# Last attention: key sums between the key blocks, four-tile scores, triangles on GpSimd and scalings on VectorE

## The chip, the cores and the metric

The kernel runs on one core of one Trainium2 chip. The metric is the device time of one execution in microseconds, as the median of several runs; lower is better. The engines are called as in the profile: PE (TensorE's matmuls) with PEld (its weight loads), DVE (VectorE), ACT (ScalarE), POOL (GpSimd) and SP (SyncE).

## The reference

The model is a chain of eight small layers on two batches of 1024 tokens with 256 channels, in float32. The change lies in the seventh stage's attention alone, which adds to the residual stream `x` a local attention of 16 heads of 64 channels. Each query block of 128 tokens sees its own and the two neighbouring key blocks, within 127 tokens, and besides them 64 "side" keys, each the sum of 16 consecutive tokens. The softmax has an extra logit of zero.

```python
bl = LOCAL_RADIUS + 1            # 128
nb = L // bl                     # 8 blocks
G = L // TOKENS_PER_BLOCK        # 64 sums of 16 tokens
q = einsum('bld,dhk->blhk', x, Wq) / sqrt(dh)
k = einsum('bld,dhk->blhk', x, Wk)
v = einsum('bld,dhk->blhk', x, Wv)
g = einsum('bld,lg->bgd', x, one_hot)          # sums of 16 tokens
side_k = einsum('bgd,dhk->bghk', g, Wk)
side_v = einsum('bgd,dhk->bghk', g, Wv)
k_cat = concatenate([three_blocks(k), side_k])
v_cat = concatenate([three_blocks(v), side_v])
logits = einsum('bnqhd,bnkhd->bnhqk', qb, k_cat)
valid = (abs(rel) <= 127) & (k_pos >= 0) & (k_pos < L)
logits = logits + where(valid, 0, -1e9)        # side keys: no bias
m = maximum(max(logits), 0)
p = exp(logits - m) / (sum(exp(logits - m)) + exp(-m))
y = einsum('bnhqk,bnkhd->bnqhd', p, v_cat)
out = einsum('blhk,hkd->bld', y, Wo)
```

A query and a key at the same place of neighbouring blocks are 128 apart and so not valid. Hence for one query, of the two neighbour blocks together, exactly 127 keys count: those after its place in the block before, and those ahead of its place in the block behind. The kernel uses that: it merges both neighbours into one block of 128 columns.

## The kernel before

The whole program is one stream of instructions written in Python; a scheduler of the language orders the instructions of each engine by when it thinks their inputs are ready, so their order on an engine isn't quite that of the text. `attn1` runs the last attention once for each batch, in two stages.

*Projection.* For each of eight groups `m` of 128 channels (two heads), `pq` holds the keys of 512 tokens (L1499) and ACT copies it to `kT` (L1500). The 64 key sums are a product of their own, `pg`, from the summed tokens `g` (L1505), copied to `sk`. Then come the values `pv` (L1513), copied to `v` by DVE and ACT in turn, and the value sums `sv` (L1527). In the second batch the steps of the next stage's adapter (`adapter2_steps`) run beside the keys.

*Heads.* `attn1_heads` walks over items `(n, m)`: eight query blocks `n`, and in each four items of two pairs of heads. `staggered` issues for each item `scores`, for the item before it `turn`, and for the one before that `values`. Twice in eight items a block of PE work stands between: `queries` projects the queries of two blocks (L1565), and DVE scales them into `qT` (L1572); `output` applies the output weights (L1689).

- `scores`, per pair of heads: both heads lie in the upper and lower 64 rows. A product of 64x128 weights with 384 keys each (L1598), one with the 64 sums each (L1602), in the PSUM tile `ps`, one bank a head. In inner blocks (`0 < n < 7`) DVE merges the neighbours with a predicated copy of 128x128 for each head (L1604, L1605, mask `near`). One instruction of DVE adds the mask `wbs`, negates and takes the row's minimum (L1608); ACT takes the exponential and its sum (L1618). With the extra logit (L1622) DVE forms the reciprocal (L1624, L1625). DVE scales the first head of the pair (L1626) and ACT the second (L1627).
- `turn`: PE transposes the probabilities into `pt` (own block, merged neighbours; L1640) and `pts` (sums; L1641). ACT copies the own block (L1644) and the sums (L1650). In inner blocks DVE splits the merged neighbours by multiplying `pt` with each of two triangles `tri` (L1647).
- `values`: products with `v` and `sv` for each head on 128x64 tiles (L1667), a copy on ACT (L1679).

PSUM in the heads' stage: `ps` twice two banks, `pt0`, `pt1`, `pts` and `py` one bank each, eight in all.

Of the kernel before, what the change touches and what calls it, by code (L numbers as in the profile page):

```python
# [9 lines left out]
F32 = mybir.dt.float32  # L10
# [8 lines left out]
P = 128  # L19
# [43 lines left out]
def tiles(tc, **how):  # L63

    return tc.tile_pool(reuse_waits="tile", **how)
# [1355 lines left out]

def load_attn1(k, pool, names):
    for n in names:
        k.w1a[n] = pool.tile([P, 2048], F32, name=f"w1a{n}")
        k.nc.sync.dma_start(out=k.w1a[n], in_=part(k.ins["w1a"], W1A, n))


def attn1(k, ci, x):
# [7 lines left out]
    with tiles(tc, name="a1r", bufs=1) as rp:  # L1436
# [6 lines left out]
        wbs = rp.tile([P, 4, G + 2 * P + G], F32, name="wbs")  # L1443
# [12 lines left out]
        left, right = slice(G, G + P), slice(G + P, G + 2 * P)  # L1456
        for t, op, sign in (
            (wbs[:, 0, right], ALU.is_gt, -1),
            (wbs[:, 1, right], ALU.not_equal, 1),
            (wbs[:, 2, left], ALU.not_equal, 1),  # L1460
            (wbs[:, 3, left], ALU.is_gt, 1),
        ):
            nc.gpsimd.affine_select(
                out=t, in_=t, compare_op=op, fill=-1.0e9, base=0, pattern=[[sign, P]], channel_multiplier=-sign
            )

        near = rp.tile([P, 2, P], U8, name="near")
        for i, t in enumerate((wbs[:, 3, left], wbs[:, 0, right])):
            nc.vector.tensor_scalar(near[:, i], t, 0.0, None, ALU.is_ge)
        for b in range(B):  # L1470
            kT = rp.tile([P, 8, S], F32, name="kT")
            v = rp.tile([P, NB, 1024], F32, name="v")

            g = rp.tile([P, 2, 2, G], F32, name="g")
            sk = rp.tile([P, 8, G], F32, name="sk")

            sv = rp.tile([P, 8, 2, 64], F32, name="sv")
            nc.gpsimd.memset(sv, 0.0)
            for c in range(2):
                nc.vector.reduce_sum(  # L1480
                    g[:, c, 0, :], ci[:, c, b * S : (b + 1) * S].rearrange("p (g t) -> p g t", t=16), axis=AX.X
                )
            nc.vector.tensor_copy(g[:, :, 1, :], g[:, :, 0, :])
            with ExitStack() as st:
                pp = st.enter_context(tiles(tc, name="a1a", bufs=2 if b else 3, space=PSUM))
# [6 lines left out]
                for m in range(8):  # L1492
                    ms = slice(m * P, (m + 1) * P)
                    for half in range(2):
                        ts = slice(b * S + half * CK, b * S + (half + 1) * CK)
                        ls = slice(half * CK, (half + 1) * CK)
                        pq = pp.tile([P, CK], F32, name="pq")
                        for c in range(2):
                            nc.tensor.matmul(pq, lhsT=wk[:, c, ms], rhs=ci[:, c, ts], start=c == 0, stop=c == 1)  # L1499
                        nc.scalar.copy(kT[:, m, ls], pq)  # L1500
                    if beside:
                        next(beside[m // 4])
                    pg = pp.tile([P, G], F32, name="pg", bufs=1 if b else 2)
                    for c in range(2):
                        nc.tensor.matmul(pg, lhsT=wk[:, c, ms], rhs=g[:, c, 0, :], start=c == 0, stop=c == 1)  # L1505
                    nc.vector.tensor_copy(sk[:, m, :], pg)
                for half in range(2):
# [17 lines left out]
                    for i in range(2):  # L1525
                        rows = slice(i * G, (i + 1) * G)
                        nc.vector.tensor_copy(  # L1527
                            sv[rows, 4 * half : 4 * half + 4, i],
                            pv[rows].rearrange("p (m i d) -> p m i d", i=2, d=64)[:, :, i],
                        )  # L1530
            with (
# [4 lines left out]
                attn1_heads(k, b, x, ci, kT, v, sk, sv, (wbs, near, tri), rp, sp, pp, yp)  # L1536


def attn1_heads(k, b, x, ci, kT, v, sk, sv, masks, rp, sp, pp, yp):
# [18 lines left out]
    def queries(n):  # L1558

        qT = rp.tile([P, 8, 2 * P], F32, name="qT", bufs=2)  # L1560
        for m in range(0, 8, 4):
            pq = pp.tile([P, 4, 2 * P], F32, name="ps")
# [9 lines left out]
            nc.vector.tensor_scalar_mul(qT[:, m : m + 4, :], pq, 0.125)  # L1572
        rows["qT", n // 2] = qT

    def scores(it):
# [5 lines left out]
        k0 = max(0, n - 1) * P  # L1581
        nk = 3 * P if inner(n) else 2 * P
        hps = [slice(64 * i, 64 * i + 64) for i in range(2)]

        keys = (slice(3 * P - nk, 3 * P), slice(G, G + nk))
        sums = (slice(3 * P, 3 * P + G), slice(0, G))
        used = (slice(P, P + W), slice(0, W))
        it["pe"] = []  # L1590
        for pair in range(2):
# [4 lines left out]
            qs = [rows["qT", n // 2][hp, m + pair, (n % 2) * P : (n % 2 + 1) * P] for hp in hps]  # L1596
            for i, hp in enumerate(hps):
                nc.tensor.matmul(  # L1598
                    ps[:, i, keys[i]], lhsT=qs[i], rhs=kT[hp, m + pair, k0 : k0 + nk], start=True, stop=True
                )  # L1600
            for i, hp in enumerate(hps):
                nc.tensor.matmul(ps[:, i, sums[i]], lhsT=qs[i], rhs=sk[hp, m + pair, :], start=True, stop=True)  # L1602
            if inner(n):
                nc.vector.copy_predicated(ps[:, 0, 2 * P : 3 * P], near[:, 0], ps[:, 0, 0:P])  # L1604
                nc.vector.copy_predicated(ps[:, 1, G : G + P], near[:, 1], ps[:, 1, G + 2 * P : G + 3 * P])  # L1605
            for i in range(2):

                nc.vector.tensor_tensor_reduce(  # L1608
                    out=pe[:, i],
                    in0=ps[:, i, used[i]],  # L1610
                    in1=wbs[:, 0 if n == 0 else 3 if n == NB - 1 else 1 + i, (1 - i) * G : (1 - i) * G + W],
# [4 lines left out]
                    accum_out=nm[:, i : i + 1],  # L1616
# [342 lines left out]
```

## Time and profile before

| | |
|---|---|
| median of 3 runs | 1522.83 us (1522.0 to 1526.31) |
| profiled execution | 1529.71 us, span 1528.0 us |
| mean granted clock of TensorE | 0.949 |
| PE busy | 1428.8 us, 94% |
| DVE busy | 873.6 us, 57% |
| ACT busy | 681.2 us, 45% |
| POOL busy | 180.7 us, 12% |
| L1598, products of queries with keys | 512 records, 110.1 us busy |
| L1608, mask and minimum | 256, 118.6 us, 487 ns each |
| L1647, triangles | 96, 64.8 us, 675 ns each |
| L1626 / L1627, scalings on DVE / ACT | 128 each, 48.8 / 70.8 us |
| L1604 / L1605, predicated copies | 96 each, 27.9 / 28.4 us |

Busy time is the union of an engine's records; a mean is that of a record. A float32 product leaves two records (two passes), each with its own weight load. Records of one engine can overlap, so the distance between two starts says more about an engine's pace than the length of a record. The times in the profile are microseconds from the start of the span.

### The profile page before, as it was taken

How to read it: one execution, taken by the hardware profiler on the slowest of the kernel's cores; microseconds unless marked ns; L12 is line 12 of the kernel's file. 1: busy time of each engine (PE TensorE's matmuls, PEld its weight loads, DVE VectorE, ACT ScalarE, POOL GpSimd, SP SyncE). 2: the span in 40 equal slices, each digit the busy share in tenths (PEclk: the TensorE clock that was granted, in tenths of full speed). 3: DMA queues.
4: the chain of work that ended last, by engine and by line, in shares of the span. 5: the costliest groups of instructions: out<-in, count | busy, mean ns of one | idle time of the engine just before them, and what ended most of it. 6: DMA issues, size and time to landing. Idle time of an engine off the chain costs nothing. (4 is left out here: it accounts for less than half of the span.)

```text
span 1528.0 us, 27342 instructions
## 1 busy us (share of the span) xinstructions
PE 1428.8 (94%) x10778; PEld 973.6 (64%) x10778; DVE 873.6 (57%) x2774; ACT 681.2 (45%) x1681; POOL 180.7 (12%) x167
## 2 busy tenths in 40 slices
PE   5998989999699999968999989999999999999998
PEld 2445977455556666645666544788887557888866
DVE  3545733121399931157887712788784237878764
ACT  2343143222122222217888721666565427656733
POOL 1523630022411121110000010000000000000011
PEclk8799578999889999979999999999999999999999
DMA  9500003300243432030000020000000000000001
GB/s 302 189 1 2 5 2 118 159 30 30 82 149 131 140 111 98 18 121 1 2 2 2 1 84 0 2 2 2 1 2 2 0 1 2 2 1 2 2 14 42
DMA packets 42757, 70.75 MB, mean 46 GB/s; under 512 B 7168, under 2 KB 35840, under 8 KB 39552
## 3 DMA queue, kind: packets, MB, share of 16 engines
q1 hardware_dynamic: 35776, 55.55, 10.8%
q0 software_dynamic: 3072, 8.65, 1.6%
q10 hardware_dynamic: 3776, 4.75, 0.9%
q8 instruction: 86, 1.41, 0.4%
q14 instruction: 47, 0.39, 0.1%
HBM read 45.09 MB, written 23.86 MB: 45 GB/s over the span
## 5 line engine op out<-in xcount | busy, mean ns | idle before, releaser
L1618 ACT ACTIVATE pe<-pe,nm 128x320 f32<-128x320 f32 x256 | 141.9, 555 | 131.1 <-DVE nm L1608 131.0
L1608 DVE CUSTOM_DVE_ANT_0 pe<-ps,wbs 128x320 f32<-128x320 f32 x256 | 118.6, 487 | 6.1 <-PE ps L1602 1.8
L1230 ACT ACTIVATE pe<-pe,nm 128x256 f32<-128x256 f32 x256 | 110.4, 498 | 20.6 <-DVE nm L1220 20.6
L965 PE MATMUL ph<-xt,w 128*128 128x512 f32 x256 | 114.0, 603 | 2.7 <-ACT xt L960 2.7
L1598 PE MATMUL ps<-kT,qT 64*128 64x384 f32 (+1 forms) x512 | 110.1, 498 | 3.3 <-DVE qT L1572 2.9
L973 PE MATMUL po<-w,h 128*128 128x256 f32 x512 | 111.8, 379 | 0.0
L973 PEld LDWEIGHTS po<-w,h 128*128 128x128 f32 x512 | 97.3, 190 | 16.6 <-issue 3.3
L1220 DVE CUSTOM_DVE_ANT_0 pe<-ps,lc 128x256 f32<-128x256 f32 x256 | 94.2, 417 | 21.1 <-PE ps L1204 19.5
L1667 PE MATMUL py<-ptt,v 128*64 128x128 f32 x1408 | 103.6, 277 | 0.1
L895 DVE SCALAR_TENSOR_TENSOR lc<-iok,idx,lc 128x256 f32<-128x256 f32 x248 | 102.1, 474 | 0.3
L965 PEld LDWEIGHTS ph<-xt,w 128*128 128x128 f32 x256 | 48.7, 193 | 62.8 <-issue 55.9
L1667 PEld LDWEIGHTS py<-ptt,v 128*64 128x64 f32 x1408 | 78.7, 137 | 11.1 <-issue 8.1
L1640 PE MATMUL pt<-ident,pe 128*128 128x128 f32 x512 | 79.8, 281 | 1.9 <-DVE pe L1626 0.9
L1239 PE MATMUL ptp<-ident,pe 128*128 128x128 f32 x512 | 73.7, 282 | 5.7 <-DVE pt L1243 3.6
L1239 PEld LDWEIGHTS ptp<-ident,pe 128*128 128x128 f32 x512 | 55.5, 141 | 33.5 <-ACT pe L1230 17.2
L968 ACT ACTIVATE h<-ph,vecs 128x512 f32<-128x512 f32 x64 | 44.0, 687 | 71.3 <-PE ph L965 71.3
L1627 ACT ACTIVATE pe<-pe,rd 128x320 f32<-128x320 f32 x128 | 70.8, 558 | 9.0 <-DVE rd L1625 8.9
L1602 PEld LDWEIGHTS ps<-sk,qT 64*128 64x128 f32 x512 | 50.9, 187 | 26.2 <-issue 0.3
L1499 PE MATMUL pq<-c,w1ak 128*128 128x512 f32 x128 | 60.1, 612 | 5.5 <-ACTq L1844 5.5
L1647 DVE TENSOR_TENSOR ptt<-pt,tri 128x512 f32<-128x512 f32 x96 | 64.8, 675 | 0.0
L1640 PEld LDWEIGHTS pt<-ident,pe 128*128 128x128 f32 x512 | 56.2, 141 | 10.9 <-issue 2.0
L976 DVE TENSOR_TENSOR ye<-po,b 128x256 f32<-128x256 f32 x32 | 13.4, 418 | 82.0 <-PE po L973 82.0
(355 smaller groups left out, 2769.8 us busy)
## 6 DMA issues: line engine op xcount, KB each, us to landing
w<-in_mw SPq DMA_DIRECT2D x16, 1024.0 KB, 5.5
xs<-z SPq DMA_DIRECT2D x8, 1088.0 KB, 11.7
ys<-z SPq DMA_DIRECT2D x4, 1024.0 KB, 11.6
xe<-xs SPq DMA_DIRECT2D x7, 544.0 KB, 6.2
more<-xs SPq DMA_DIRECT2D x7, 544.0 KB, 3.9
x<-in_xT ACTq DMA_DIRECT2D x4, 512.0 KB, 5.9
g<-ys ACTq DMA_DIRECT2D x4, 512.0 KB, 5.9
out_x<-o SPq DMA_DIRECT2D x8, 256.0 KB, 2.1
```

Source lines behind the costliest of these rows:

```text
L895: nc.vector.scalar_tensor_tensor(n, key, k.idx[:, qb, j : j + 1], n, ALU.is_equal, ALU.add)
L965: nc.tensor.matmul(ph, lhsT=w1[:, c, m * P : (m + 1) * P], rhs=xt[:, c, :], start=c == 0, stop=c == 1)
L973: nc.tensor.matmul(po, lhsT=h[:, m, j * P : (j + 1) * P], rhs=w2[:, m, :], start=m == 0, stop=m == 7)
L1220: nc.vector.tensor_tensor_reduce(out=pe[:, j, :], in0=it["ps"][i][:, j, :], in1=k.lc[:, q0 + j, :], scale=-1.0, scalar=3.0e38, op0=ALU.add ...
L1230: nc.scalar.activation(pe[:, j, :], pe[:, j, :], AF.Exp, bias=nm, scale=-1.0)
L1239: nc.tensor.transpose(ptp[:, kb, j, :], it["pe"][i][:, j, kb * P : (kb + 1) * P], k.ident)
L1598: nc.tensor.matmul(ps[:, i, keys[i]], lhsT=qs[i], rhs=kT[hp, m + pair, k0 : k0 + nk], start=True, stop=True)
L1608: nc.vector.tensor_tensor_reduce(out=pe[:, i], in0=ps[:, i, used[i]], in1=wbs[:, 0 if n == 0 else 3 if n == NB - 1 else 1 + i, (1 - i) * G ...
L1618: nc.scalar.activation(pe[:, i], pe[:, i], AF.Exp, bias=nm[:, i : i + 1], scale=-1.0, accum_out=den[:, i : i + 1])
L1627: nc.scalar.activation(pe[:, 1], pe[:, 1], AF.Copy, scale=rd[:, 1:2])
L1640: nc.tensor.transpose(pt[1 - j if i and inner(n) else j][:, 2 * pair + i, :], pe[:, at : at + P], k.ident)
L1667: nc.tensor.matmul(py[64 * i : 64 * i + 64, (m + pair) % 4, :], lhsT=keys[:, hs], rhs=it["pts"][:, pair, :] if j == 3 else it["pt"][:, j, ...
```

## The change

Five things are changed together.

1. *Layout of the keys.* `kT` holds 1280 columns for 1024 keys: between the key blocks lie copies of the 64 key sums, three in the rows of the first head of each pair and four in those of the second (`KEYS`). For every query block one contiguous stretch holds the keys it needs and one copy of the sums. A head's view has the sums in the middle or at an edge; `window(n)` gives for both heads where the stretch starts, which columns are used and which are merged into which (`place`, `merge`, `kind`, `masked`, `parts`).
2. *Key sums.* The product `pg` goes. DVE sums `pq` over 16 tokens into `sk`, and GpSimd copies `sk` into its places in `kT`, once every four groups. The copies of `pq` to `kT` are split at the gaps: ACT copies the first head's 64 rows, DVE the second's.
3. *Scores.* Each pair has four products: two heads by two halves of 64 queries, each on a tile of 64x64, with 320, 384 or 448 columns. A half of the queries leaves out the 64 columns of a neighbour in which it has no valid key. The products with the sums go. In inner blocks the predicated copy of 128 columns becomes two of 64 columns, one on all rows and one on 64 rows.
4. *Triangles.* ACT copies the merged block from `pt[1]` as it is; GpSimd multiplies the copy with each triangle in SBUF.
5. *Scalings.* DVE scales both heads of a pair; ACT none.

Besides, `qT` becomes three buffers of four groups in place of two of eight, the `pq` tile has three buffers in both batches, `wbs` has three masks in place of four, and `sv` is held twice, with its two halves exchanged, since which head's sums come first now depends on the block.

The diff, cut to its core:

```diff
+class Keys:
+    def __init__(self, order):
+        self.at, self.sums, at = {}, [], 0
+        for n in order:
+            if n is None:
+                self.sums.append(at)
+                at += S // 16
+            else:
+                self.at[n] = at
+                at += P
...
+KEYS = [Keys([0, 1, None, 2, 3, None, 4, 5, None, 6, 7]), Keys([None, 0, 1, 2, None, 3, 4, None, 5, 6, 7, None])]
+
+def window(n):
+    first = 0 if n == 0 or n in (1, 3, 5) else 1
+    return [KEYS[i].view(i, n, first ^ i) for i in range(2)]
...
-                        nc.scalar.copy(kT[:, m, ls], pq)
+                        gs = slice(half * G // 2, (half + 1) * G // 2)
+                        nc.vector.reduce_sum(sk[:, m, gs], pq.rearrange("p (g t) -> p g t", t=16), axis=AX.X)
+                        for i in range(2):
+                            hp = slice(64 * i, 64 * i + 64)
+                            for n0, n1 in KEYS[i].runs(4 * half, 4 * half + 4):
+                                at, w = KEYS[i].at[n0], (n1 - n0) * P
+                                o = (n0 - 4 * half) * P
+                                copy = nc.vector.tensor_copy if i else nc.scalar.copy
+                                copy(kT[hp, m, at : at + w], pq[hp, o : o + w])
...
-                    for c in range(2):
-                        nc.tensor.matmul(pg, lhsT=wk[:, c, ms], rhs=g[:, c, 0, :], start=c == 0, stop=c == 1)
-                    nc.vector.tensor_copy(sk[:, m, :], pg)
+                    if m % 4 == 3:
+                        for i in range(2):
+                            hp = slice(64 * i, 64 * i + 64)
+                            for at in KEYS[i].sums:
+                                nc.gpsimd.tensor_copy(kT[hp, m - 3 : m + 1, at : at + G], sk[hp, m - 3 : m + 1])
...
                     for i in range(2):
-                        rows = slice(i * G, (i + 1) * G)
-                        nc.vector.tensor_copy(
-                            sv[rows, 4 * half : 4 * half + 4, i],
...
+                        for j in range(2):
+                            rows = slice((i ^ j) * G, ((i ^ j) + 1) * G)
+                            nc.vector.tensor_copy(
+                                sv[rows, j, 4 * half : 4 * half + 4, i],
...
-            for i, hp in enumerate(hps):
-                nc.tensor.matmul(
-                    ps[:, i, keys[i]], lhsT=qs[i], rhs=kT[hp, m + pair, k0 : k0 + nk], start=True, stop=True
-                )
-            for i, hp in enumerate(hps):
-                nc.tensor.matmul(ps[:, i, sums[i]], lhsT=qs[i], rhs=sk[hp, m + pair, :], start=True, stop=True)
-            if inner(n):
-                nc.vector.copy_predicated(ps[:, 0, 2 * P : 3 * P], near[:, 0], ps[:, 0, 0:P])
-                nc.vector.copy_predicated(ps[:, 1, G : G + P], near[:, 1], ps[:, 1, G + 2 * P : G + 3 * P])
+            for half in range(2):
+                qs = slice((n % 2) * P + half * 64, (n % 2) * P + half * 64 + 64)
+                for hp, view in zip(hps, views):
+                    c0, c1 = view.parts[half]
+                    nc.tensor.matmul(
+                        ps[hps[half], view.head, c0:c1],
+                        lhsT=rows["qT", n // 2, m // 4][hp, (m + pair) % 4, qs],
+                        rhs=kT[hp, m + pair, view.start + c0 : view.start + c1],
+                        start=True,
+                        stop=True,
+                    )
+            for view in views:
+                i, j = view.head, view.place
+                if inner(n):
+                    to, of = view.merge
+                    both, one = (slice(0, 64), slice(64, P)) if view.kind == 0 else (slice(64, P), slice(0, 64))
+                    for rs, cs in ((slice(0, P), both), (one, one)):
+                        nc.vector.copy_predicated(
+                            ps[rs, i, to + cs.start : to + cs.stop],
+                            near[rs, view.kind, cs],
+                            ps[rs, i, of + cs.start : of + cs.stop],
+                        )
...
-            nc.vector.tensor_scalar_mul(pe[:, 0], pe[:, 0], rd[:, 0:1])
-            nc.scalar.activation(pe[:, 1], pe[:, 1], AF.Copy, scale=rd[:, 1:2])
+            for j in range(2):
+                nc.vector.tensor_scalar_mul(pe[:, j], pe[:, j], rd[:, j : j + 1])
...
         if inner(n):
-            for i in range(2):
-                nc.vector.tensor_mul(ptt[:, 1 + i], pt[1], tri[:, i : i + 1, :].to_broadcast([P, 4, P]))
+            nc.scalar.copy(ptt[:, 1], pt[1])
+            for i in (1, 0):
+                nc.gpsimd.tensor_mul(ptt[:, 1 + i], ptt[:, 1], tri[:, i : i + 1, :].to_broadcast([P, 4, P]))
```

## The prediction

> **What bounds the kernel now.** The page comes first, for the engines' shares:
>
> ```profile
> PE 1428.8 (94%) x10778; PEld 973.6 (64%) x10778; DVE 873.6 (57%) x2774; ACT 681.2 (45%) x1681; POOL 180.7 (12%) x167
> ```
>
> PE looks like the bound, but these are means over all stages. The change lies in the last attention, from 890 to 1465 us, so I read one steady step there (two pairs of heads), first PE in the timeline:
>
> ```profile
> 1319.94 0.92 PE L1598 MATMUL ps<-kT,qT 64*128 64x384 f32 x4
> 1320.68 0.34 PE L1602 MATMUL ps<-sk,qT 64*128 64x64 f32 x4
> 1320.85 0.87 PE L1598 MATMUL ps<-kT,qT 64*128 64x384 f32 x4
> 1321.55 0.33 PE L1602 MATMUL ps<-sk,qT 64*128 64x64 f32 x4
> 1321.82 0.65 PE L1640 MATMUL pt<-ident,pe 128*128 128x128 f32 x4
> ...
> 1324.96 0.92 PE L1598 MATMUL ps<-kT,qT 64*128 64x384 f32 x4
> ```
>
> The columns are start, length, engine, line, tiles, count. A step takes PE 5.02 us (1319.94 to 1324.96) without a gap: scores 1.88, transposes 1.24, values 1.90. Now DVE over the same time:
>
> ```profile
> 1321.38 0.29 DVE L1604 COPY_PREDICATED ps<-near,ps 128x128 f32<-128x128 uint8 x1
> ...
> 1324.49 0.67 DVE L1647 TENSOR_TENSOR ptt<-pt,tri 128x512 f32<-128x512 f32 x1
> 1325.08 0.38 DVE L1626 TENSOR_SCALAR pe<-pe,rd 128x320 f32<-128x320 f32 x1
> 1325.37 0.68 DVE L1647 TENSOR_TENSOR ptt<-pt,tri 128x512 f32<-128x512 f32 x1
> 1326.01 0.16 DVE L1624 TENSOR_TENSOR rd<-den,extra 128x2 f32<-128x2 f32 x1
> 1326.41 0.39 DVE L1626 TENSOR_SCALAR pe<-pe,rd 128x320 f32<-128x320 f32 x1
> 1326.71 0.28 DVE L1604 COPY_PREDICATED ps<-near,ps 128x128 f32<-128x128 uint8 x1
> ```
>
> One turn of DVE takes 5.33 us (1321.38 to 1326.71), longer than PE's step. DVE falls behind 0.31 us a step and is saved because after every four steps PE works 7.1 us on queries (L1565) or 7.5 on the output (L1689), where DVE catches up. Four steps and such a block are a "burst": two bursts took 55.28 us (1297.38 to 1352.66), one 27.64.
>
> When does DVE decide? PE's transposes in a burst's fourth step need the third turn of DVE. With a turn D, DVE starting L after the burst, then 0.15 hand-over, 0.62 transposes of the last pair, 1.90 values, 7.3 block and 0.26 (half of the 0.52 us after each query block), a burst lasts L + 3D + 10.23. With L = 1.13 (scores at 1314.92, first copy at 1316.05) and D = 5.33 that is 27.35, only 0.29 below the measured 27.64. **PE bounds the bursts, but DVE stands right behind it.**
>
> **The change part by part.**
>
> *Scores.* The products with the key sums (L1602) go; the four products of a pair now lie on four 64x64 tiles. A quarter tiling already runs:
>
> ```profile
> 144.86 0.34 PE L412 MATMUL sc<-ru,k 64*64 64x64 f32 x8 [0.15 <-DVE A L420]
> ```
>
> Eight records of 0.22 to 0.27 us fit in 0.34, so four run at once. A pass of 384 columns takes 0.32 us; two passes a pair, two pairs, first load and the switch to transposes (0.15) make 1.5 to 1.6 us against 1.88. I take 0.35 saved, a PE step of 4.67. In blocks 1 and 6 a tile has 448 columns (0.05 longer a pass, 0.2 a step), which doesn't matter if DVE bounds. In blocks 0 and 7 (320 columns) some 0.25 is saved a step; no triangles lie there, and of these 16 steps in all I leave out four that only fill the pipe: 12 x 0.25 = 3 us.
>
> *DVE's turn.* Starts lie apart as follows: L1647 0.59 and 0.64, L1626 0.30, predicated copies 0.325. The triangles go: -1.23. Two scalings come from ACT: +0.60. Four copies of 128 columns become eight of 64: 64 elements fewer are 0.067 less at the 1.04 ns an element of DVE's rows (128x512 0.68, 128x256 0.42), so 8 x 0.26 = 2.08 against 1.30: +0.78 (ends: 8 x 0.20, +0.3; 8 x 0.325, +1.3). D = 5.33 - 1.23 + 0.60 + 0.78 = 5.48. L becomes 0.90 (no sums to wait for). Burst: 0.90 + 16.44 + 10.23 = 27.57. PE alone would do 27.64 - 4 x 0.35 = 26.24, so **the 1.4 us that PE gains stay hidden behind DVE**: -0.07 a burst.
>
> Half of those copies' views start at row 64. Row first: the two sv copies (L1527), rows 0 and 64, start 0.43 us apart though the first is 0.416 long, while 256-wide products (L463) start 0.335 apart at 0.419 long. [...]
>
> *POOL.* Two products of 128x512 per step, in SBUF, come after an ACT copy. Nearest rows: L309, in place, 1.09 us; L202 1.26. Together about 2.2 us, one behind the other. In themselves they are free: PE has the values of the step before, the next scores and transposes (about 4.7 us) to do before it needs them, against 0.5 + 2.2. What they cost is DVE:
>
> ```profile
> 1473.40 1.40 POOL L223 TENSOR_TENSOR both<-nsq 128x512 f32<-128x512 f32 x1 [101.06 <-ACT nsq L221]
> 1473.72 3.31 DVE L1731 SCALAR_TENSOR_TENSOR xk<-df,vecs,c 128x512 f32<-128x512 f32 x2
> 1474.76 1.72 POOL L202 TENSOR_TENSOR both<-x 128x512 f32<-128x512 f32 x1
> 1476.44 2.34 POOL L1755 TENSOR_TENSOR ka<-ka 128x1024 f32<-128x1024 f32 x1
> 1476.95 3.04 DVE L1731 SCALAR_TENSOR_TENSOR xr<-df,vecs,c 128x512 f32<-128x512 f32 x2
> ```
>
> These DVE instructions take 0.74 us alone. Beside POOL two took 3.31 and the next 2.38: each waited for POOL's running product, ran 0.55, and POOL took the next turn. DVE rows that read PSUM and one SBUF tile (L308 beside L309, 0.74) show nothing of it. Which of ours are exposed? By the row, those with two SBUF inputs: the additions L1624, two a step; that is W = 0.3 us a turn at most. [...] The closest the trace has is L497, a copy in SBUF: 0.54 alone, 1.17 beside a POOL memset. [...]
>
> When do they meet? In the turn that starts at 1321.38, ACT copied ptt at +2.4, behind the exponentials. The raw copy follows 0.5 to 1 later, and POOL works from about +3.4 to +5.6. DVE's scalings lie at +3.7 and +5.0, its second addition at +4.6: in the window. One scaling that meets a product waits the better part of 1.1 us; in turn-taking a second may. Ends for the wait W a turn: 0 and 2.2. I take 0.9, one hit. Behind the waiting scaling queue the next scores' copies and L1608; ACT's exponentials and PE's transposes wait for those. Burst: 0.90 + 3 x 6.38 + 10.23 = 30.27, +2.63. Twelve bursts (24 inner steps a batch, two batches): **+31.6 us**.
>
> *ACT* loses two scalings (-0.90) and gets a copy (+0.46); it idles in the bursts, so nothing.
>
> *Projection.*
>
> ```profile
> 897.97 0.55 PE L1505 MATMUL pg<-g,w1ak 128*128 128x64 f32 x4
> 898.36 3.65 PE L1499 MATMUL pq<-c,w1ak 128*128 128x512 f32 x8
> ```
>
> pg holds PE 0.39 us (897.97 to 898.36); 16 of them go: **-6.5 us** with the second batch's somewhat longer ones. In return DVE gets, per 512 columns, a sum (0.61) and copies of 384 and 128 (0.48 and 0.22, by length from 0.69 for 512): 1.31 against PE's 1.72, and ACT two copies of 256 (0.25 each) for one of 0.47. PE covers it; the second batch's adapter adds 10 us to DVE and as much to PE. If that cover failed the 6.5 would be lost. POOL copies the sums, 14 a batch of 64x256, some 0.6 each by half of L309: 8 us beside 30 us of value products. Four more sv copies a batch, 0.42 each, end beside the first queries. No DMA is added or moved; nothing changes on SP's queue.
>
> *Sum:* 31.6 - 6.5 - 3 = +22. The profiled execution took 1529.71 us (span 1528.0), 6.9 above the median 1522.83 of three runs; I put the sum on the median: **1545 us**.
>
> **Rivals.** (1) *Faster: the lock is missed.* If POOL's products fall under DVE's copies and L1608 (1.9 us a pair, which read PSUM), W is 0: 12 x -0.07 - 9.5 = -10, 1512; with copies at 0.20 (D = 5.0, burst 26.24 by PE) -26, 1497. It decides from W = 0.29 down (12 x 3W = 10.3). For it: the static order may part them. Against: the positions above, and that a late DVE delays transposes, raw copy and POOL alike, so the meeting repeats. (2) *Both products hold DVE*: W = 2.0, +71 - 9.5, 1585. (3) *The tiles don't run at once*: twice the passes, scores 2.9, PE step 6.0, burst 31.6: +48 - 9.5, about 1560. Against: L412.
>
> **How the numbers follow.** The lock with about one hit (W 0.45 to 1.6, 1528 to 1570) 0.61; rival 1 0.20; rival 2 0.09; rival 3 0.04; a W near 0.3, which ends within 0.3% (4.6 us, about what a measurement here can tell from none) 0.06. Slower 0.74, same 0.06, faster 0.20. Range 1508 to 1580: half of rival 1 and half of rival 2 stay outside.
>
> **What would show it.** Right: scalings of 320 columns beside POOL longer than 0.38 us, up to 1.5; steps over 5.3 us within bursts; PE waiting on DVE pe in the transposes; PE's busy share down; kT stage 3 us shorter a batch. Wrong: scalings at 0.38 throughout, PE steps of 4.7, or four score products a pair one behind another.

## The result and the profile after

The changed kernel takes 1587.11 us (median of 6 runs, 1585.22 to 1591.38) against 1523.49 us for the kernel before on the same chip: a ratio of 1.040, 95% interval 1.038 to 1.043. It is slower, as forecast, but by 63.6 us where the forecast said 22, and it lies 7 us above the upper end of the range. The profiled execution has a span of 1583.5 us at a granted clock of 0.96, no lower than the 0.949 of before. The two profiled spans lie only 55.5 us apart, because in the execution before the stages ahead of this attention took longer: its first key product starts at 889.1 us, here at 880.2.

First the page, engine shares:

```profile
PE 1415.0 (89%) x10714; PEld 905.8 (57%) x10714; DVE 1008.3 (64%) x3086; ACT 650.5 (41%) x1633; POOL 314.7 (20%) x290
```

PE has 14 us less to do and its share falls from 94% to 89%; DVE has 135 us more. Then the groups of instructions by line (busy, mean ns, and idle time before them with what ended it); the last one is of before:

```profile
L1720 POOL TENSOR_TENSOR ptt<-ptt,tri 128x512 f32<-128x512 f32 x96 | 123.7, 1289 | 393.0 <-ACT ptt L1718 389.2
L1712 PE MATMUL pt<-ident,pe 128*128 128x128 f32 x512 | 87.3, 290 | 51.5 <-DVE pe L1698 38.1 <-DVE rd L1695 10.7 <-ACT yT L1752 1.6
L1695 DVE TENSOR_TENSOR rd<-den,extra 128x2 f32<-128x2 f32 x128 | 63.8, 499 | 5.7 <-ACT extra L1693 2.7
```

```profile
L1640 PE MATMUL pt<-ident,pe 128*128 128x128 f32 x512 | 79.8, 281 | 1.9 <-DVE pe L1626 0.9 <-ACT ptt L1644 0.7
```

L1712 are the transposes: PE now stands still for 51.5 us ahead of them (1.9 us before, L1640), nearly all until a scaling (L1698) or an addition (L1695) of DVE is done. An addition adds two numbers to two numbers in each row (`den` and `extra`), and takes 499 ns in the mean. The view of one tile's instructions has the shortest, median and longest duration, and shows that this mean is made of two kinds:

```profile
L1698 DVE TENSOR_SCALAR pe<-pe,rd x256: 371/384/1476, 953.9 to 1509.4; 128x320 f32<-128x320 f32 x128
L1695 DVE TENSOR_TENSOR rd<-den,extra x128: 140/160/1283, 953.2 to 1508.7; 128x2 f32<-128x2 f32 x128
```

Most are as short as before (there at most 164 and 389 ns); 47 additions and 29 scalings are far longer. What they exceed the median by is 43.8 us for the additions and 26.1 us for the scalings. The timeline of DVE and of POOL shows what the long ones wait for:

```profile
1360.53 1.14 DVE L1695 TENSOR_TENSOR rd<-den,extra 128x2 f32<-128x2 f32 x1
...
1361.90 0.68 DVE L1698 TENSOR_SCALAR pe<-pe,rd 128x320 f32<-128x320 f32 x2
...
1367.65 1.71 DVE L1698 TENSOR_SCALAR pe<-pe,rd 128x320 f32<-128x320 f32 x2
1369.28 1.26 DVE L1695 TENSOR_TENSOR rd<-den,extra 128x2 f32<-128x2 f32 x1
```

```profile
1359.03 2.62 POOL L1720 TENSOR_TENSOR ptt<-ptt,tri 128x512 f32<-128x512 f32 x2 [4.22 <-ACT ptt L1718]
1367.77 2.76 POOL L1720 TENSOR_TENSOR ptt<-ptt,tri 128x512 f32<-128x512 f32 x2 [6.12 <-ACT ptt L1718]
```

The addition of 1360.53 ends at 1361.67, POOL's two products at 1361.65. Two scalings from 1367.65 take 1.71 us instead of 0.68, across the first product of the second pair; the addition behind them ends at 1370.54, the second product at 1370.53. So it is in the whole stage: of the instructions that started well inside a product, all 45 additions and all 20 scalings lasted to its end, and no copy, reduction or reciprocal got longer (at most 240, 493 and 168 ns). This hold is the "lock" of the forecast and the expectations. Meanwhile PE:

```profile
1362.43 0.64 PE L1712 MATMUL pt<-ident,pe 128*128 128x128 f32 x4 [0.96 <-DVE pe L1698]
```

Its transposes wait 0.96 us for the scaling behind the held addition.

Where the time went: from the first score to the last, the two batches take 229.2 and 231.4 us, 33.0 and 32.7 us more than before. Key projection and the stretch between the batches are 1.6 us shorter together. The turn of DVE and the burst explain the heads. I take the turn from the start of a step's first predicated copy to the next step's, as the mean of the three turns between two blocks, over the ten full bursts of both batches, and the burst from the first copy behind one block to the first behind the next:

| kernel | turn of DVE, us | burst, us | median, us | ratio to before, 95% interval |
|---|---|---|---|---|
| before | 5.36 | 27.73 | 1523.49 | |
| the change | 7.18 | 33.22 | 1587.11 | 1.040 (1.038 to 1.043) |

The rest of a burst, beside three turns, is 11.66 us before and 11.69 after, so the forecast's form, a constant and three turns, holds for these two kernels to 0.03 us. Twelve bursts by 5.49 us are 65.9 us, and the heads grew by 65.7. So all of it is in DVE's turn, 1.82 us longer. In the runs that follow the rest lies between 11.5 and 12.6 us: there the time has to be read from the burst, and a turn alone doesn't give it.

### The profile page after: what moved, and what is told of

Its sections match the earlier page's. It is cut to its first block, busy times and chain, and to the rows that moved or that the text cites. A ratio compares the mean times of both kernels' runs of the same rounds, so it can differ in the third digit from the quotient of the medians.

```text
span 1583.5 us, 27601 instructions
## 1 busy us (share of the span) xinstructions
PE 1415.0 (89%) x10714; PEld 905.8 (57%) x10714; DVE 1008.3 (64%) x3086; ACT 650.5 (41%) x1633; POOL 314.7 (20%) x290
## 5 line engine op out<-in xcount | busy, mean ns | idle before, releaser
L1720 POOL TENSOR_TENSOR ptt<-ptt,tri 128x512 f32<-128x512 f32 x96 | 123.7, 1289 | 393.0 <-ACT ptt L1718 389.2
L1712 PE MATMUL pt<-ident,pe 128*128 128x128 f32 x512 | 87.3, 290 | 51.5 <-DVE pe L1698 38.1
L1679 DVE CUSTOM_DVE_ANT_0 pe<-ps,wbs 128x320 f32<-128x320 f32 x256 | 119.3, 486 | 6.2 <-PE ps L1659 2.3
L1659 PE MATMUL ps<-kT,qT 64*64 64x384 f32 (+2 forms) x1024 | 107.7, 493 | 11.5 <-DVE nm L1679 5.0
L1712 PEld LDWEIGHTS pt<-ident,pe 128*128 128x128 f32 x512 | 54.7, 141 | 109.3 <-DVE pe L1698 42.1
L1698 DVE TENSOR_SCALAR pe<-pe,rd 128x320 f32<-128x320 f32 x256 | 113.1, 484 | 3.8
L1740 PE MATMUL py<-ptt,v 128*64 128x128 f32 x1408 | 109.2, 286 | 1.1 <-POOL ptt L1720 1.1
L1740 PEld LDWEIGHTS py<-ptt,v 128*64 128x64 f32 x1408 | 84.2, 142 | 13.2 <-issue 11.4
L1672 DVE COPY_PREDICATED ps<-near,ps 64x64 f32<-64x64 uint8 (+1 forms) x384 | 80.3, 227 | 9.2 <-PE ps L1659 0.5
L977 POOL DMA_INDIRECT ys<-ye,row x32 | 31.8, 995 | 211.6 <-DVE ye L976 211.6
L1695 DVE TENSOR_TENSOR rd<-den,extra 128x2 f32<-128x2 f32 x128 | 63.8, 499 | 5.7 <-ACT extra L1693 2.7
```

What stands on the lines that cost most here:

```text
L1659: nc.tensor.matmul(ps[hps[half], view.head, c0:c1], lhsT=rows["qT", n // 2, m // 4][hp, (m + pair) % 4, qs], rhs=kT[hp, m + pair, view.sta ...
L1672: nc.vector.copy_predicated(ps[rs, i, to + cs.start : to + cs.stop], near[rs, view.kind, cs], ps[rs, i, of + cs.start : of + cs.stop],)
L1679: nc.vector.tensor_tensor_reduce(out=pe[:, j], in0=ps[:, i, view.used : view.used + W], in1=wbs[:, 0 if inner(n) else 1 + view.kind, o : o ...
L1698: nc.vector.tensor_scalar_mul(pe[:, j], pe[:, j], rd[:, j : j + 1])
L1712: nc.tensor.transpose(to[:, 2 * pair + view.head, :], pe[:, at : at + P], k.ident)
L1720: nc.gpsimd.tensor_mul(ptt[:, 1 + i], ptt[:, 1], tri[:, i : i + 1, :].to_broadcast([P, 4, P]))
```

## The experiments

All runs, with the same measures; each ratio is to the kernel before on the same chip, whose medians were 1521.8 to 1525.7 us. The turns here are means; those that the expectations name were read from single turns and can lie 0.3 us off.

| run | turn | burst | median | ratio, 95% interval |
|---|---|---|---|---|
| e1 change without triangle products | 5.90 | 29.27 | 1541.37 | 1.011 (1.007 to 1.014) |
| e6 before, idle products on POOL | 6.30 | 30.46 | 1557.08 | 1.020 (1.017 to 1.024) |
| e2 change, additions by column | 6.54 | 31.80 | 1573.83 | 1.032 (1.029 to 1.036) |
| e3 change, second scaling on ACT | 6.43 | 31.83 | 1572.21 | 1.034 (1.030 to 1.038) |
| e4 change, triangles on DVE | 6.21 | 30.77 | 1555.60 | 1.022 (1.019 to 1.025) |
| e5 scores and layout alone | 5.81 | 29.93 | 1547.82 | 1.016 (1.012 to 1.020) |
| e8 as e5, one copy a head | 5.86 | 29.14 | 1534.80 | 1.009 (1.005 to 1.012) |
| e10 as e8, triangles on POOL | 6.06 | 30.24 | 1554.71 | 1.021 (1.018 to 1.024) |
| e14 before, copies between | 5.88 | 29.15 | 1541.85 | 1.012 (1.008 to 1.016) |
| e12 as e8, copies first | 5.33 | 27.53 | 1517.37 | 0.995 (0.993 to 0.997) |
| e16 as e12, two more scalings on ACT | 5.00 | 27.05 | 1520.96 | 0.997 (0.995 to 0.999) |
| e13 change, copies first | 7.03 | 33.53 | 1594.25 | 1.046 (1.042 to 1.050) |
| e15 as e1, copies first | 5.74 | 29.68 | 1545.70 | 1.012 (1.010 to 1.015) |
| e17 as e5, copies first | 6.02 | 30.33 | 1551.30 | 1.016 (1.014 to 1.019) |

**e1: the products taken away.**

```diff
             nc.scalar.copy(ptt[:, 1], pt[1])
-            for i in (1, 0):
-                nc.gpsimd.tensor_mul(ptt[:, 1 + i], ptt[:, 1], tri[...])
```

The values then read the raw copy for both neighbours (an edit not shown here), so the result is not that of the model.

> The changed kernel with both triangle products left out: the values of both neighbour blocks are multiplied with the raw copy of the merged block, so that part of the computation is missing. POOL has no work in the heads' stage, all else stays. Theory L (POOL's products hold VectorE's two-operand additions and its scalings under a lock, 1.46 us a turn as summed from the changed kernel's trace): the waits go, the turn of VectorE falls to 5.5 us, a burst to 27.6, and the time to about 1519 us (1510 to 1530). Rival R (the longer list of VectorE instructions and the new order of the instructions cost the time, POOL has little to do with it): above 1550 us.

Measured 1541.37 us: of the 63.6 us some 46 go with the products, and no addition or scaling is long any more (at most 164 and 390 ns). But some 16 to 18 us stay, which neither theory had. The end of a turn in its timeline of DVE, and the same instructions of a step's first pair before:

```profile
1359.27 0.16 DVE L1695 TENSOR_TENSOR rd<-den,extra 128x2 f32<-128x2 f32 x1
1359.46 0.17 DVE L1696 RECIPROCAL rd<-rd 128x2 f32<-128x2 f32 x1
1359.67 0.68 DVE L1698 TENSOR_SCALAR pe<-pe,rd 128x320 f32<-128x320 f32 x2
```

```profile
1323.93 0.15 DVE L1624 TENSOR_TENSOR rd<-den,extra 128x2 f32<-128x2 f32 x1
1324.00 0.48 DVE L1608 CUSTOM_DVE_ANT_0 pe<-ps,wbs 128x320 f32<-128x320 f32 x1
1324.41 0.16 DVE L1625 RECIPROCAL rd<-rd 128x2 f32<-128x2 f32 x1
```

In e1 addition, reciprocal and scaling stand one behind the other, each needs the result of the one ahead, and they start 0.19 and 0.21 us apart. Before, a reduction stood between addition and reciprocal and a triangle (at 1324.49) behind the reciprocal; the next instruction started 0.07 and 0.08 us after each of them.

**e6: the products alone, on the kernel before.** Two products of the same size a step, whose result nobody reads.

```diff
         nc.scalar.copy(ptt[:, 0], pt[0])
         if inner(n):
+            idle = sp.tile([P, 4, P], F32, name="idle", bufs=1)
+            for i in range(2):
+                nc.gpsimd.tensor_mul(idle, ptt[:, 0], tri[...])
```

> The kernel before with one thing added: in inner blocks POOL multiplies ACT's copy of the own block with both triangles into a tile that nobody reads, two products of 128x512 a step, as in the changed kernel. Nothing waits for POOL but the release of the copy's buffer. Theory L: VectorE's additions and its one scaling a pair meet the products; W about 1.2 us a turn, a burst 27.35 + 3.6 = 31, 12 x 3.3 = +40, about 1563 us (1545 to 1575), and additions of over 1 us in the trace. Rival R (the price was the new chain ACT, POOL, PE, or VectorE's list): no change, 1521 to 1526 us.

Measured 1557.08 us: work that nobody waits for costs about 31 us. The timelines of DVE and POOL:

```profile
1325.41 0.67 DVE L1650 TENSOR_TENSOR ptt<-pt,tri 128x512 f32<-128x512 f32 x1
1326.00 0.85 DVE L1626 TENSOR_SCALAR pe<-pe,rd 128x320 f32<-128x320 f32 x1
1326.77 0.68 DVE L1650 TENSOR_TENSOR ptt<-pt,tri 128x512 f32<-128x512 f32 x1
1327.38 0.66 DVE L1624 TENSOR_TENSOR rd<-den,extra 128x2 f32<-128x2 f32 x1
```

```profile
1325.39 2.63 POOL L1648 TENSOR_TENSOR idle<-ptt,tri 128x512 f32<-128x512 f32 x2 [3.64 <-ACT ptt L1644]
```

The scaling is 0.47 us too long, the addition 0.50, and it ends at 1328.04, when POOL ends (1328.02). The triangles L1650, which read PSUM and one tile in SBUF, take 0.67 and 0.68 us beside POOL as they do without it. The turn grows by 0.94 us. Nobody uses the result of these products, so it is the hold on DVE that costs, not a longer way from ACT over POOL to PE.

**e2 and e3: which instructions wait.** In e2 the addition is two instructions of one column, with one input and a column as scalar; in e3 the second scaling goes back to ACT.

```diff
-            nc.vector.tensor_add(rd, den, extra)
+            for j in range(2):
+                nc.vector.tensor_scalar_add(rd[:, j : j + 1], den[:, j : j + 1], extra[:, j : j + 1])
```

> The changed kernel with the addition of den and extra (two operands in SBUF) done as two one-column additions whose second operand is a per-partition scalar. Theory L1 (each VectorE instruction loses for itself, and the additions lost 43.8 of 69.9 us): the additions' waits go, about 33 us of the time with them, about 1555 us. Theory L2 (whatever stands first in VectorE's queue waits for the product, and the scalings 0.4 us behind the addition wait in its place): 1575 to 1590, and the scalings' waits grow from 26 us to 50 or more. R: 1590 (only 0.13 us more an addition).

Measured 1573.83 us, 12 or 13 us less than the change. In the view of the tiles the additions no longer wait, at most 217 ns:

```profile
L1699 DVE TENSOR_SCALAR pe<-pe,rd x256: 370/381/1428, 949.0 to 1495.9; 128x320 f32<-128x320 f32 x128
L1696 DVE TENSOR_SCALAR rd<-den,extra x256: 191/204/217, 947.8 to 1495.1; 128x1 f32<-128x1 f32 x128
```

But the scalings behind them do: 55 are long, and together 35.0 us over the median, against 26.1 in the change. The wait is partly handed on to the next instruction that the products hold. Neither expectation fits: the gain is little more than a third of that of L1, and the scalings' waits grew by 9 us, not to 50.

```diff
-            for j in range(2):
-                nc.vector.tensor_scalar_mul(pe[:, j], pe[:, j], rd[:, j : j + 1])
+            nc.vector.tensor_scalar_mul(pe[:, 0], pe[:, 0], rd[:, 0:1])
+            nc.scalar.activation(pe[:, 1], pe[:, 1], AF.Copy, scale=rd[:, 1:2])
```

> The changed kernel with the second head's scaling back on ACT. Two exposed scalings a turn in place of four, and 0.6 us less for VectorE. The kernel without triangles had a turn of 5.87 us, so 5.27 here, plus a wait W for POOL. If every exposed instruction waits for itself (two additions, two scalings: W about 1.2): burst 0.90 + 3 x 6.5 + 10.23 = 30.6, about 1553 us (1545 to 1565). If the additions, which come first in each tail, take all of the wait (W as in the changed kernel, 1.46): 1562 us.

Measured 1572.21 us, 10 us or more above both figures: with half of the scalings the long ones' sum is 29.3 us for the scalings and 13.5 for the additions, 42.8 in place of 69.9. But another wait took their place:

```profile
L1695 DVE TENSOR_TENSOR rd<-den,extra 128x2 f32<-128x2 f32 x128 | 33.7, 264 | 38.1 <-ACT extra L1693 36.7
```

DVE stood still for 36.7 us ahead of the additions until ACT had the extra logit, 2.7 us in the change. ACT does 128 scalings more here, of 0.56 us each; that these delay it is likely, but no run separates it. The rest of a burst is 12.5 us.

**e4 and e5: the rest without POOL.** e4 is the change with the triangles on DVE; e5 also has the second scaling on ACT, so only layout and scores are left of the change.

```diff
-            nc.scalar.copy(ptt[:, 1], pt[1])
-            for i in (1, 0):
-                nc.gpsimd.tensor_mul(ptt[:, 1 + i], ptt[:, 1], tri[...])
+            for i in range(2):
+                nc.vector.tensor_mul(ptt[:, 1 + i], pt[1], tri[...])
```

> The changed kernel with the triangles back on VectorE from PSUM, both scalings still on VectorE; no POOL products, no lock. VectorE's turn is 5.87 + 1.23 = 7.1 us, or 6.7 if the products again fill the gaps in the chain addition, reciprocal, scaling. Theory L: burst 31.2 to 32.4, 1560 to 1575 us, so the move to POOL would cost some 12 to 25 us net of the lock. If VectorE's list did not matter: below 1545.

> Only the layout, the sums and the scores of the change: triangles on VectorE from PSUM and the second head's scaling on ACT, as before. No lock. VectorE's turn is 5.33 + 0.78 (eight copies of 64 columns for four of 128) = 6.11 us, a burst 0.90 + 3 x 6.11 + 10.23 = 29.5 against 27.64. Theory V (VectorE bounds the bursts, PE's shorter scores gain nothing): 12 x 1.8 - 5 = +17, about 1540 us (1530 to 1550). Rival P (PE bounds, its 0.35 us a step count): about 1505 us.

Measured 1555.60 and 1547.82 us. So moving the triangles to POOL cost some 30 us (63.6 us over the kernel before against 33.8), and even the scores and layout alone lose 22 to 24, less than half of it by a longer rest of the burst (12.5 us). Set e4 beside e1: the triangles, 1.23 us a turn, make DVE's turn 0.31 us longer (6.21 against 5.90) and the whole 18 us, where 36 turns by 1.23 us would be 44. More than half of what was taken off DVE came back as other time. The scheduler also orders the rest of e4 differently (a copy stands between addition and reciprocal, at 1309.01), so this is the price of triangles and order together.

**e8 and e10: one copy a head.** Full-width products (448 columns in every inner block) let one 128-column predicated copy do for a head.

```diff
-                    c0, c1 = view.parts[half]
+                    c0, c1 = 0, view.parts[1][1]
...
-                    for rs, cs in ((slice(0, P), both), (one, one)):
-                        nc.vector.copy_predicated(ps[rs, i, ...], near[rs, view.kind, cs], ps[rs, i, ...])
+                    nc.vector.copy_predicated(ps[:, i, to : to + P], near[:, view.kind], ps[:, i, of : of + P])
```

> The change's layout, sums and scores with triangles on VectorE and the second scaling on ACT, as before, and besides one predicated copy of 128 columns a head as before; all four score products then take the full 448 columns (0.2 us a step of PE). VectorE's turn is back at 5.33 us, PE's step about 4.9. Theory V: the eight small copies were what made the scores' change slow by itself (1547.8); burst 27.0 to 27.2, 1512 to 1520 us. Rival (the new order of the instructions costs it): above 1530.

> As the kernel with one copy and full width, but triangles by POOL from ACT's raw copy, and the addition as two one-column additions with a per-partition scalar, which POOL doesn't hold. Exposed are only two scalings a turn. VectorE's turn 5.33 - 1.23 + 0.13 = 4.2, plus W of 0.5 to 1.0: below PE's step of 4.9. Theory: PE bounds again, burst 27.0, 1505 to 1520 us, no slower than with the triangles on VectorE. If one scaling a pair still costs a whole product each turn (W 1.3 and more): 1525 to 1540.

Both missed: e8 took 1534.80 us. In the heads' inner blocks it has DVE's instructions of the kernel before, one for one, and yet a turn of 5.86 us. e10, as e8 with POOL's products and additions by column, took 1554.71; its scalings have a median of 640 ns and a longest of 1462, where the kernel before has 385 and 389; that these are the same waits for products is likely. What e8 has changed on DVE is only the order.

**e14 and e12: the order.** The change writes copy, reduction, copy, reduction for the two heads of a pair; before, both copies came first. e14 puts the order of the change into the kernel before:

```diff
-            if inner(n):
-                nc.vector.copy_predicated(ps[:, 0, 2 * P : 3 * P], ...)
-                nc.vector.copy_predicated(ps[:, 1, G : G + P], ...)
             for i in range(2):
+                if inner(n) and i == 0:
+                    nc.vector.copy_predicated(ps[:, 0, 2 * P : 3 * P], ...)
+                if inner(n) and i == 1:
+                    nc.vector.copy_predicated(ps[:, 1, G : G + P], ...)
                 nc.vector.tensor_tensor_reduce(...)
```

> The kernel before with nothing changed but the order in which one pair's instructions are written: copy, reduction, copy, reduction, as the change writes them. Theory O: the step's last reduction and addition fall behind the triangles, some 0.8 us a turn of DVE is exposed, bursts 29.3 to 29.8 instead of 27.64, 12 of them: 1540 to 1550 us. Rival T: the order of copies is free, 1521 to 1526 us.

and e12 puts the order of before into e8:

```diff
                     nc.vector.copy_predicated(ps[:, i, to : to + P], ...)
+            for view in views:
+                i, j = view.head, view.place
                 o = P + G - view.masked
                 nc.vector.tensor_tensor_reduce(...)
```

> As the run with one 128-column predicated copy a head (change's key layout and score products, triangles on DVE, second scaling on ACT), but the two copies of a pair are written ahead of the two score reductions, as in the kernel before, instead of copy, reduction, copy, reduction. DVE then keeps the order of before: the last reduction of a step stands ahead of the two triangles, and the 0.81 us for which its addition waited for ACT's exponential lies under the triangles. Theory O (the order is what is left of the loss): DVE's turn goes from 6.17 back to 5.33 us, bursts from 29.2 to 27.1 or 27.4, the whole to 1510 to 1522 us. Rival T (the new score products themselves cost it, as tiles or waits for a PSUM tile): it stays above 1530 us.

Measured 1541.85 and 1517.37 us: the same instructions in the other order cost 17.6 us on the kernel before, and setting it right gains 17.4 us on e8 (1.3% by the two ratios). e14's DVE timeline:

```profile
1303.83 0.48 DVE L1608 CUSTOM_DVE_ANT_0 pe<-ps,wbs 128x320 f32<-128x320 f32 x1
...
1305.14 0.16 DVE L1624 TENSOR_TENSOR rd<-den,extra 128x2 f32<-128x2 f32 x1 [0.82 <-ACT extra L1622]
...
1305.41 0.28 DVE L1605 COPY_PREDICATED ps<-near,ps 128x128 f32<-128x128 uint8 x1
```

and e12's:

```profile
1312.33 0.48 DVE L1677 CUSTOM_DVE_ANT_0 pe<-ps,wbs 128x320 f32<-128x320 f32 x1
...
1313.40 0.38 DVE L1695 TENSOR_SCALAR pe<-pe,rd 128x320 f32<-128x320 f32 x1
1313.69 0.68 DVE L1717 TENSOR_TENSOR ptt<-pt,tri 128x512 f32<-128x512 f32 x1
1314.33 0.16 DVE L1693 TENSOR_TENSOR rd<-den,extra 128x2 f32<-128x2 f32 x1
```

The step's last reduction starts a chain through ACT: the exponential, the extra logit, and only then the addition. In e12 the two triangles (at 1312.81 and 1313.69) and a scaling lie in that gap, and the addition finds its input ready. In e14 the scheduler put the last reduction behind the triangles; nothing is left for the gap, and DVE stands still for 0.82 us with the next step's copies queued behind. Summed over all additions, before and then in e14:

```profile
L1624 DVE TENSOR_TENSOR rd<-den,extra 128x2 f32<-128x2 f32 x128 | 20.2, 158 | 5.6 <-ACT extra L1622 4.8
```

```profile
L1624 DVE TENSOR_TENSOR rd<-den,extra 128x2 f32<-128x2 f32 x128 | 20.0, 156 | 41.8 <-ACT extra L1622 40.6
```

The same view gives 32.5 us for e8 and 5.1 for e12. **In these four kernels the triangles are cover for ACT's chain where they stand behind the last reduction, and none where they stand ahead of it.** The change and e1 don't lose their time here: their additions wait 2.7 and 4.5 us for ACT. e12 beats the kernel before by 0.5%, with the new score tiles and key layout, one copy a head and the triangles left where they were.

**e16: what bounds e12.**

```diff
-            nc.vector.tensor_scalar_mul(pe[:, 0], pe[:, 0], rd[:, 0:1])
+            if pair == 0:
+                nc.vector.tensor_scalar_mul(pe[:, 0], pe[:, 0], rd[:, 0:1])
+            else:
+                nc.scalar.activation(pe[:, 0], pe[:, 0], AF.Copy, scale=rd[:, 0:1])
```

> As the run with the copies first, and of the second pair of a step both scalings on ACT. If DVE's turn (5.33) still decides a burst there, it falls to 5.03 and the time by up to 0.9 us a burst, 11 us, until PE's step of 4.95 decides (27.1 a burst): 3 to 8 us less than the run with the copies first. If PE decides already, no difference within 2 us. If ACT, with 0.47 us more a step, becomes late, it is slower.

Measured 1520.96 us, no gain. The turn fell to 5.00 us as expected and the bursts by 0.48, 5.8 us in twelve; but the first six steps of the batches, up to the first full burst, took 36.5 and 36.4 us in place of 32.2 and 33.9 and gave it back. Why those steps are longer is open. e16 lies 0.3% below the kernel before.

**e13, e15 and e17: copies first in the other versions.** The edit is e12's, on the change, on e1 and on e5.

> The whole change, but the copies of both heads of a pair are written ahead of their reductions. Theory O with the lock as it was: DVE's own turn shrinks from 5.87 towards 5.5 us, and the waits for POOL stay about 1.46 us a turn: 7 to 14 us less than the change, 1573 to 1580 us. Rival: the waits for POOL depend on where the additions and scalings stand, so a new order meets more or less of the products: anything from 1545 to 1600 us, with the long instructions' sum moving by more than 15 us.

> The change without its two triangle products (the values read the raw copy for both neighbours, so that part of the computation is left out), and with the copies of both heads of a pair ahead of their reductions. Theory O (the 16 us that stayed when the products went are the order's): DVE's turn goes from 5.87 to the forecast 5.4 or 5.5 us, bursts from 29.3 to 27.4 or 27.8, the whole to 1520 to 1530 us. Theory C (they are the eight small copies): the turn stays above 5.7, the time within 4 us of 1541.

> The change's score products and key layout with eight 64-column copies a step, triangles on DVE and second scaling on ACT, but the copies of both heads ahead of their reductions. By the sum for eight copies DVE's turn is 5.33 + 0.78 = 6.11 us and a burst 0.8 + 18.3 + 10.2 = 29.3: 1537 to 1544 us, a few us less than with copy and reduction in turn (1547.82), and 20 us or more above the run with one copy a head and the copies first (1517.37). If the order was the whole loss and small copies cost nothing, 1517 to 1523 us.

All three miss the theory of the order. e13 is slower than the change, 1594.25 us. Its scalings now stand where the products run; DVE's and POOL's timelines:

```profile
1319.26 2.56 DVE L1700 TENSOR_SCALAR pe<-pe,rd 128x320 f32<-128x320 f32 x2
```

```profile
1319.02 2.62 POOL L1722 TENSOR_TENSOR ptt<-ptt,tri 128x512 f32<-128x512 f32 x2 [10.33 <-ACT ptt L1720]
```

Two scalings take 2.56 us for 0.68: each waits for one product. The scalings' excess is 62.1 us, the additions' 18.6, 80.7 in place of 69.9. The sum moved with the order, as the rival said, though by 11 us and not by over 15.

e15 keeps 1545.70 us, a little more than e1. That looks like the theory of the small copies, but the timeline shows another loss: where no triangles are left on DVE, a good order has nothing to put into the gap, and the addition waits for ACT here too (0.26 us at 1317.34, elsewhere up to 0.57 us, 19.6 us in all against 4.5 in e1). The turn is still shorter than e1's, but the rest of a burst is 12.4 us for 11.6. e17 took 1551.30 us, 34 us more than e12, from which it differs by the small copies (eight of 64 columns for four) and the narrower products. So the small copies cost their part; how much of the 34 us is theirs and how much the order that the scheduler made around them is open.

## Why the prediction was right and wrong

*Right.* The direction, and the mechanism that decided: DVE stands behind PE in the bursts, three turns of DVE set the length of a burst, and POOL's products hold DVE's two-input additions (up to 1.28 us for 0.16) and its scalings (up to 1.48 for 0.38), both from SBUF to SBUF: e13's two scalings take 2.56 us over two products of 2.62, while the reductions of the change, from PSUM (L1679), take at most 0.49 us. The four tiles run at once: unstalled, a step's eight score products, 16 passes, take 1.52 us (at 1378.69), like the 1.5 to 1.6 of the sum. PE's gain is hidden, as said: its busy time fell and the time rose. Every sign that the forecast listed for "right" came, but for the kT stage.

*Wrong: the sizes, term by term.*

1. **The wait W, "I take 0.9, one hit".** The turn with products is 7.18 us, without 5.90 (e1): W = 1.28 us. By 36 turns that is 14 us of the miss. That a scaling waits for a product no run ahead of the forecast shows; by its nearest row, a copy in SBUF (L497), the hit was the author's estimate. The runs show it: 29 of the change's 256 scalings are long, 26.1 us in all, and none is in e1, without the products. The size of a hit was right, their number wasn't: over the 48 inner steps 76 instructions are long, 1.6 a step in place of one, by 0.92 us each. The forecast listed the additions as exposed, but priced them at "W = 0.3 us a turn at most" and took one hit, of a scaling. That price is about twice their own 0.16 us, but the wait has nothing to do with that length: an addition waits for the product, up to 1.28 us, and the additions' excess alone is 43.8 us, 0.91 us a step. What bounds the wait here is how many such instructions meet a product, by the product's length. The products were sized low as well, "together about 2.2 us"; the two take 2.6.

2. **The turn D, "5.33 - 1.23 + 0.60 + 0.78 = 5.48".** Measured without the products 5.90, 0.42 more, by 36 turns 15 us. In a turn of e1 (1302.96 to 1308.82) the copies take 1.84, +0.54 for the forecast +0.78, and the four scalings 1.43, +0.83 for +0.60: together what was forecast. The failed step is "The triangles go: -1.23". Without them additions and reciprocals take 0.80 us where they took 0.55, and the gaps around the reductions are 0.13 longer, so that only 0.85 of the 1.23 is gained. The triangles did not only take time, they stood between instructions that depend on each other (the lines under e1). e4 against e1, where the order of the rest differs too, gives even less, 0.31. The sum treated DVE's turn as a list of durations, and said nothing of the order in which the scheduler would put them.

3. **L, "becomes 0.90 (no sums to wait for)", and the block's 10.23.** The part of a burst beside the turns was 11.69 us where the formula had 11.13, and the formula was low for the kernel before too (11.36 against 11.66). The forecast took its growth from the measured 27.64 of before, not from the formula's own 27.35, and so lost the difference. Some 0.5 us by twelve bursts, 6 us.

4. **Projection, "-6.5", and "3 us" in blocks 0 and 7.** The key stage (first key product to first value product) is 0.5 us shorter in the first batch (32.56 to 32.02) and 1.9 in the second, where the forecast had 3 each; some of that is lost again behind it, so that 0.5 and 1.1 us remain. In e12 and ten other runs with the same stage the first batch's takes 30.5 to 30.6; what lies between 32.0 and 30.5 is open. As the heads grew by twelve bursts' worth, the 3 us of blocks 0 and 7 did not come either. Together 8 us.

The four make 43 us; the forecast was 41.6 short. Rival 2 named nearly the right time, 1585, for another reason, which is luck: it had the turn at 5.48 + 2.0, and the truth was 5.90 + 1.28.

*Left open.* How the 16 to 18 us of e1 divide between the small copies, four scalings and the exposed chain. Item 2 divides one turn by its trace, but no run separates them: e15 and e17 tried it by the order alone, and the scheduler made new orders. Open is also why the rest of a burst differs by up to 1 us between the runs.

## What to carry to other kernels

Before work is moved off the engine that decides, look at what stands around it in its timeline. An instruction that lies between a result and its use, on the same engine or by way of another, is cover for that chain, and taking it away gives back only what the chain doesn't need (here 18 us of 44, e4 against e1). A two-input addition or a wide scaling of VectorE in SBUF that met a product of GpSimd in SBUF waited to its end, however short it was by itself (0.16 us became up to 1.28, 0.38 up to 1.48); count such meetings by the product's length, and price them in one run with an idle product on the old kernel (e6). After taking one wait away, look for the next: in e3 the wait for ACT took the place of the hold. Where a scheduler orders the instructions, two lines written the other way around can be worth 17 us of 1520; compare the order of the deciding engine's instructions before comparing their durations.

## What the runs showed that was not expected

- The 128x2 addition with two inputs lasted up to 1.28 us, the same addition as two one-column instructions with a scalar column never above 0.217 us beside the same products; the scalings, with a scalar column too but 320 columns wide, lasted up to 1.43 us in that run. Reciprocals of 128x2, also in SBUF, never got longer (at most 0.168 us).
- Products that nobody reads cost 31 us on the kernel before (e6).
- The start row of a predicated copy shows, for which the forecast's sum has no term. Four 64-column copies in a row, of two pairs, take DVE 0.62 us in block 6 of the change (at 1458.77), where all start at row 0, 0.75 in block 2 (1325.49), where the start row changes once, and 0.88 in block 3 (1364.55), where it changes twice: 0.13 us a change, by the kernel's text and these lengths.
- Four fp32 products on 64x64 tiles run at once in this kernel: 16 passes of 384 columns in 1.52 us, where the scores before took 1.88 with the sums. It is worth little here because DVE stands behind PE: with one copy a head and the order kept (e12) the whole gains 0.5%.
